# A graph layer on one core: the loop's buffers take fixed homes shared with the front, and the first one-hot matrices are built while the list goes through DRAM

## The chip, the cores and the metric

The kernel runs on one core of one Trainium2 chip. The metric is device time in microseconds of a whole execution. The engines are named as the profile names them: PE (matmuls; PEld loads their weights), DVE, ACT, POOL, and SP, which issues DMAs. A core has a PSUM memory of eight banks of 512 floats per partition, into which PE writes; DVE and ACT read it there. Everything else that the engines work on lies in SBUF.

## The reference

The layer takes 6250 nodes of 128 channels and 206,250 edges, sorted by their target node `dst`. It normalises the nodes, and for each node takes the largest message of its incoming edges:

```python
h = jnp.maximum(_layernorm(x, axis=-1), 0.0)
# for each edge (src, dst), with W = [W1 W2]:
feat = jnp.concatenate([h[dst], h[src] - h[dst]], axis=-1)
msg = feat @ W.T + b
out = jax.ops.segment_max(msg, dst, num_segments=6250)
x = x + jnp.where(jnp.isfinite(out), out, 0.0)
```

A message is a part that depends on `dst` alone plus a part `B[src]` that depends on `src` alone, so the kernel needs, for each node, the channelwise maximum of `B` over its neighbours.

## The kernel before

Nodes are numbered as `l * 50 + q`, with 125 values of `l` and `Q` = 50 of `q`. The lanes are the 128 partitions; a lane owns `LD` = 49 successive target nodes and looks at a window of `WIN` = 1792 edges. All order is written out by hand: the engines run their instructions in the order in which the code names them, and each engine waits, by semaphores, for the others where an instruction touches what another one wrote or read.

**The front** (lines 168 to 723) loads the windows, and does two things at once. It computes `B` (the small steps `turn`, `product` and `remainder` of `micro`, on PE and ACT, 75 in all for 25 pairs of `q`; `ln(n)` issues the next n of them), in two parts: `Bp` in SBUF, and `Bt` and `XA` in DRAM. And it marks the edges that a dense method cannot take: in the lag loop (lines 557 to 562) DVE compares the window with itself at 41 lags, and PE adds the results up in `dup`, four banks of PSUM (line 483); three result buffers `eq` take turns. `among[i]` lists what is issued after lag i. ACT takes the sign of `dup` (574), DVE scans it (585), and eleven passes (615 to 624) move the marked edges to the front of a list. `rest[i]` lists what is issued after pass i, among it `spread_a` and `spread_b` (where each lane's list goes), `turned` (PE transposes that make `TV`, `TD` and `TQ`) and `own_last`. The list is stored in DRAM as `LT` (666) and gathered back in two pieces (669, 670). What DVE does meanwhile is the product with `dup` of line 672, whose result becomes `TQ`, and tests whose results go to `badc`. Then `ridx` is made (696), and POOL begins to gather rows of `Bt` into `X`, a ring of `GB` = 12 groups.

**The way to the loop** (842 to 879). For each of 13 tiles of up to ten lanes there are two units (6 and 4 lanes). For a unit, `pieces` are six DVE comparisons and products that make one-hot matrices `OHQ` and `OHD` (755 to 762) from `TQ`, `TD` and `TV`; `mats` are 14 small PE matmuls for each two lanes, into `pv` (792). `square` (ACT, 801 to 804) makes `Vb` and `Vf` of `pv`. Before the loop stand the pieces and matmuls of units 0 and 1, `put_own(0)` (rows of `Bt`, turned by PE and copied to `acc` by ACT), `square(0)` and the pieces of unit 2.

**The loop** (937 to 974) has 325 pairs: 13 tiles of 490 columns (the last 392), with 25 pairs of `q` each. For a pair, `one_hots` makes two or three one-hot matrices: PE computes `z` (874), ACT makes `oh` of it (875). PE multiplies them with `Bp` into the pair's `ps`, two banks, with four or six matmuls (949), and DVE takes the maximum of `ps` and `acc2` into `acc2` (955). `ps` comes from a pool with two buffers (733). Beside this DVE runs the stream (159: a maximum over the gathered rows, 396 steps, a little over one in a pair), the pieces of later units, and PE the `pv` matmuls of later units, as `plan` says. The PSUM of the loop: three banks of `z`, four of `ps`, one of `pv`; that of the front: four of `dup`, two of `pt`, two of `pm`. Pools are opened for the front (170 to 172) and, after it, for the loop (732 to 734).

**The end** (983 to 996) turns `acc`, takes the maximum with the rows `R` gathered from the stream and stores the sum with x.

Of the kernel before, what the change touches and what calls it, by code (L numbers as in the profile page):

```python
# [12 lines left out]
I32 = mybir.dt.int32  # L13
# [42 lines left out]
def gnn_kernel(tc, x, src, dst, W, b, out):  # L56
# [35 lines left out]
    with ExitStack() as ctx:  # L92
# [14 lines left out]
        with ExitStack() as body:  # L107
# [30 lines left out]
            none = keep.tile([P, C], F32, name="none")  # L138

# [28 lines left out]
            with ExitStack() as pre:  # L168
                pool = pre.enter_context(tc.tile_pool(name="pre", bufs=1))
                ps_d = pre.enter_context(tc.tile_pool(name="ps_d", bufs=1, space=PSUM))  # L170
                ps_t = pre.enter_context(tc.tile_pool(name="ps_t", bufs=2, space=PSUM))
                ps_m = pre.enter_context(tc.tile_pool(name="ps_m", bufs=2, space=PSUM))
                dup = ps_d.tile([P, WIN], F32, name="dup")
# [47 lines left out]
                spare = acc[:1, 4 * GQ * C:]  # L221
# [8 lines left out]
                frow = spare[:, 256:256 + 2 * C].rearrange("o (r c) -> o r c", r=2)  # L230
# [7 lines left out]
                KA = pool.tile([P, 64 + WIN], I16, name="KA")  # L238
                KB = pool.tile([P, 64 + WIN], I16, name="KB")
                dlc_ = pool.tile([P, 64 + WIN + 2], BF16, name="dlc_")  # L240
# [40 lines left out]
                swin = pool.tile([P, WIN + 8], I32, name="swin")  # L281
                dwin = pool.tile([P, WIN], I32, name="dwin")
                big = pool.tile([P, WIN], F32, name="big")
# [33 lines left out]
                p = ps_m.tile([P, 512], F32, name="pm")  # L317
# [28 lines left out]
                kk = pool.tile([P, NS], F32, name="kk")  # L346
# [28 lines left out]
                def spread_begin():  # L375
                    p = ps_t.tile([P, 2 * P], F32, name="ptb", tag="pt")
                    T_.matmul(p[:1, :P], begin, ident, start=True, stop=True)
                    spread["p"] = p
# [14 lines left out]
                bs = spare[:, 512:512 + 3 * P - 1]  # L393
# [11 lines left out]
                def turn(k):  # L405
                    pt = ps_t.tile([P, 2, P], F32, name="pt")
# [8 lines left out]
                def product(k):  # L415
                    pm = steps[k]["pm"] = ps_m.tile([P, 2, 2 * C], F32, name="pm")
# [34 lines left out]
                vm = pool.tile([P, WIN], BF16, name="vm")  # L451
                q16 = pool.tile([P, WIN], BF16, name="q16")
                q2 = eq[2].bitcast(I16)
                gk = KB[:, 64:]
                d16 = pool.tile([P, WIN], I16, name="d16")
                s16 = pool.tile([P, WIN], I16, name="s16")
# [40 lines left out]
                own = pool.tile([P, WIN], BF16, name="own")  # L497
# [36 lines left out]

                among = {i: [] for i in range(SH + 1)}
                among[5] += [lambda: A_.copy(KB[:, 64:], KA[:, 63:63 + WIN])]
# [18 lines left out]
                for i in range(1, 35):  # L555
                    among[i].append(lambda: ln(1))
# [21 lines left out]
                less = junk[0]  # L578
                V.tensor_tensor(less[:, 1:], d16[:, 1:], d16[:, :WIN - 1], ALU.is_lt)
                V.memset(less[:, :1], 0.0)  # L580
                ln(6)
# [11 lines left out]
                def spread_a():  # L593
                    p = ps_m.tile([P, 512], F32, name="pm")
                    T_.matmul(p[:1, :P], nres, ident, start=True, stop=True)
                    V.tensor_scalar_add(rows[:, 0, :P], p[:1, :P], -float(GR))
                    V.memset(rows[:, 1], 0.0)
                    V.memset(rows[:, 4], 0.0)
                    V.tensor_tensor_scan(rows[:, 1, 2:], rows[:, 0, :P], rows[:, 4, :P], 0.0, op0=ALU.add, op1=ALU.max)
                    V.tensor_tensor(rows[:, 2, :P], lrow, rows[:, 1, 1:P + 1], ALU.subtract)  # L600
                    V.scalar_tensor_tensor(rows[:, 3, :P], lrow, float(GR - ST), rows[:, 1, :P], op0=ALU.add,
                                           op1=ALU.subtract)
                    V.tensor_scalar_max(rows[:, 3, :P], rows[:, 3, :P], 0.0)

                def spread_b():
                    p = ps_m.tile([P, 512], F32, name="pm")
                    for j, r in enumerate((2, 3, 1)):
                        o = 1 if r == 1 else 0
                        T_.matmul(p[:, j:j + 1], rows[:, r, o:o + P], ones[:1, :1], start=True, stop=True)
                    V.tensor_copy(cols_, p[:, :2])  # L610
                    V.tensor_copy(over_, p[:, 2:3])

                mask = big.bitcast(I32)

                def pass_(i):
                    s = 1 << i
                    parts = ((0, WIN - s),)
                    if s == 512:
                        parts = ((0, NS), (1024, min(1024 + NS, WIN - s)))
                    elif s == 1024:  # L620
                        parts = ((0, NS),)
                    for a, z in parts:
# [36 lines left out]
                for i in range(11):  # L659
                    pass_(i)  # L660
                    for f in rest[i]:
                        f()
# [409 lines left out]
```

## Time and profile before

| | us |
|---|---|
| median of three runs | 807.34 (806.42 to 807.71) |
| the profiled execution | 807.11 |
| its span (first to last instruction) | 805.2 |
| DVE: first lag's comparison | from 31.57 |
| ACT: first sign of `dup` | from 101.61 |
| SP: store of the list | from 147.78 |
| DVE: the gathered list is read | from 154.62 |
| PE: first `ps` matmul of the loop | from 174.45 |
| DVE: last step of the loop (965) | from 779.85 |
| mean granted clock of PE | 0.959 |

Times within the span count from its first instruction. The two us between span and execution lie around it. A row of the timeline gives start, length, engine, line, operation, output and input, and in brackets how long the engine had been idle before it and what ended that.

### The profile page before, as it was taken

How to read it: one execution, taken by the hardware profiler on the slowest of the kernel's cores; microseconds unless marked ns; L12 is line 12 of the kernel's file. 1: busy time of each engine (PE TensorE's matmuls, PEld its weight loads, DVE VectorE, ACT ScalarE, POOL GpSimd, SP SyncE). 2: the span in 40 equal slices, each digit the busy share in tenths (PEclk: the TensorE clock that was granted, in tenths of full speed). 3: DMA queues.
4: the chain of work that ended last, by engine and by line, in shares of the span. 5: the costliest groups of instructions: out<-in, count | busy, mean ns of one | idle time of the engine just before them, and what ended most of it. 6: DMA issues, size and time to landing. Idle time of an engine off the chain costs nothing.

```text
span 805.2 us, 12657 instructions
## 1 busy us (share of the span) xinstructions
PE 689.9 (86%) x3875; PEld 517.3 (64%) x3882; DVE 723.1 (90%) x1274; ACT 541.0 (67%) x1163; POOL 452.7 (56%) x489
## 2 busy tenths in 40 slices
PE   1697956579999898998989899998989999899992
PEld 0354534357677676776767677676767767677881
DVE  7999989869999888999999989999998999997976
ACT  4553467446899999567676767777776777777740
POOL 3000000377767377666667677777777777777270
PEclk9999999769999998999999999999999999999997
DMA  6420122323335833333333333433434343333385
GB/s 188 128 65 4 61 65 65 116 62 83 92 104 120 203 98 88 97 93 104 92 83 106 94 107 96 108 99 96 110 96 111 96 108 99 102 103 98 84 208 160
DMA packets 81692, 82.38 MB, mean 102 GB/s; under 512 B 11756, under 2 KB 69731, under 8 KB 81362
## 3 DMA queue, kind: packets, MB, share of 16 engines
q1 hardware_dynamic: 65741, 46.02, 20.2%
q0 software_dynamic: 15312, 34.57, 17.3%
q10 hardware_dynamic: 564, 0.92, 0.4%
q8 instruction: 32, 0.52, 0.3%
q14 instruction: 43, 0.35, 0.1%
HBM read 45.39 MB, written 39.19 MB: 105 GB/s over the span
## 4 chain that ended last, share of the span: by engine, by line
PE 56%; DVE 21%; ACT 13%; issue 6%; DMA 2%; POOL 0%; SPq 0%; DVEq 0%; ACTq 0%; POOLq 0%
PE ps L949 31%; PE z L874 14%; PE pv L792 7%; ACT oh L875 6%; DVE T L494 4%; DVE acc L955 3%; DVE dwin L624 2%; ACT Vb L802 1%; ACT dump L969 1%; ACT Vb L801 1%; DVE big L623 1%; DVE X L159 1%; ACT Vf L804 1%; DVE stats L294 1%; PE pm L420 1%
## 5 line engine op out<-in xcount | busy, mean ns | idle before, releaser
L86 POOL DMA_INDIRECT X<-Bt,ridx x396 | 393.9, 995 | 159.4 <-issue 44.8
L875 ACT ACTIVATE oh<-z 126x490 fp32r<-126x490 f32 (+1 forms) x754 | 381.1, 578 | 149.8 <-PE z L874 148.1
L949 PE MATMUL ps<-oh,Bp 126*128 126x490 f32 (+1 forms) x1508 | 445.1, 423 | 7.7 <-DVE acc L955 6.8
L955 DVE TENSOR_TENSOR acc<-acc,ps 128x980 f32<-128x980 f32 (+1 forms) x312 | 360.0, 1154 | 49.8 <-PE ps L949 45.0
L949 PEld LDWEIGHTS ps<-oh,Bp 126*128 126x128 f32 x1508 | 285.2, 192 | 107.9 <-DVE acc L955 36.4
L874 PE MATMUL z<-Vb,Sel 128*126 128x490 f16 (+1 forms) x650 | 195.8, 375 | 29.0 <-ACT oh L875 25.7
L159 DVE SCALAR_TENSOR_TENSOR X<-X,slim 128x128 f32<-128x128 f32 x395 | 136.2, 345 | 0.6
L874 PEld LDWEIGHTS <-Sel 128*126 128x126 f16 x754 | 100.6, 141 | 41.5 <-issue 6.6
L86 POOL DMA_INDIRECT swin<-LT,cols__955 x2 | 1.9, 956 | 135.6 <-DVE own_n L684 135.3
L792 PEld LDWEIGHTS <-OHQ 128*128 128x128 bf16 x910 | 62.4, 163 | 18.0 <-issue 17.2
L792 PE MATMUL pv<-OHD,OHQ 128*128 128x28 bf16 (+1 forms) x896 | 67.1, 228 | 4.6 <-DVE X L700 4.5
L86 POOL DMA_INDIRECT R<-M,last_e x49 | 47.5, 969 | 30.3 <-issue 20.5
L755 DVE TENSOR_TENSOR OHQ<-T,IQ 128x1092 bf16<-128x1092 bf16 (+5 forms) x104 | 61.6, 600 | 0.0
L483 PE MATMUL dup<-T,identb 128*128 128x512 bf16 (+1 forms) x159 | 39.4, 371 | 9.3 <-DVE T L494 8.7
L874 PE MATMUL z<-Vf,Sel 128*126 128x490 f16 (+1 forms) x104 | 38.9, 374 | 0.5 <-ACT Vf L804 0.5
L420 PE MATMUL pm<-wT,hT 128*125 128x256 f32 x100 | 30.0, 426 | 7.5 <-ACT hT L409 7.4
L969 ACT ACTIVATE dump<-lane_dl,nbias 128x472 bf16<-128x472 int32 x50 | 36.1, 721 | 0.0
L483 PEld LDWEIGHTS <-identb 128*128 128x128 bf16 x164 | 15.9, 101 | 25.4 <-issue 13.3
L420 PEld LDWEIGHTS pm<-wT,hT 128*125 128x125 f32 x100 | 19.7, 207 | 14.0 <-ACT hT L409 11.5
L403 ACT ACTIVATE hs<-X,nmr,rstd 125x128 f32<-125x128 f32 x50 | 22.1, 495 | 0.5 <-DVE nmr L306 0.5
L624 DVE COPY_PREDICATED dwin<-big,dwin 128x472 int32<-128x472 int32 (+10 forms) x12 | 21.8, 1813 | 0.4
L953 DVE TENSOR_TENSOR acc<-ps,acc 128x980 f32<-128x980 f32 (+1 forms) x13 | 15.1, 1163 | 7.7 <-PE ps L949 6.1
(266 smaller groups left out, 468.6 us busy)
## 6 DMA issues: line engine op xcount, KB each, us to landing
M<-X SPq DMA_DIRECT2D x198, 128.0 KB
X<-Bt,ridx POOLq DMA_INDIRECT x396
XA<-in_x POOLq DMA_DIRECT2D x1, 3125.0 KB
ownb<-Bt SPq DMA_DIRECT2D x12, 245.0 KB
X<-in_x SPq DMA_DIRECT2D x5, 560.0 KB
Bt<-acc SPq DMA_DIRECT2D x5, 560.0 KB
XA<-acc SPq DMA_DIRECT2D x5, 560.0 KB
out_x<-R SPq DMA_DIRECT2D x10, 224.0 KB
```

The lines of the kernel that those rows point to most:

```text
L86: G_.indirect_dma_start(out=o, out_offset=None, in_=table, in_offset=bass.IndirectOffsetOnAxis(ap=idx, axis=0))
L159: V.scalar_tensor_tensor(G[:, j], state["prev"], slim[:, k:k + 1], G[:, j], op0=ALU.min, op1=ALU.max)
L420: T_.matmul(pm[:L, j], hT[k % 2][:, j, :L], wT, start=False, stop=j == 1)
L483: T_.matmul(dup[:, c0:c1], w, e[:, c0:c1], start=first, stop=last)
L624: V.copy_predicated(pk[:, a:z], mask[:, a:z], pk[:, a + s:z + s])
L755: V.tensor_tensor(OHQ[:, :nl, a:z], over(TQ, z - a), iq, ALU.is_equal)
L792: T_.matmul(o, w, m, start=False, stop=True, skip_group_check=True)
L874: T_.matmul(z[:L + 1, :n], Sel[:, order[i // 2][j]], f[t % 2][:, :n], start=True, stop=True)
L875: A_.activation(oh[:, :n], z[:L + 1, :n], AF.Relu)
L949: T_.matmul(ps[:, j, :n], w, o[:, :n], start=m == 0, stop=m == len(todo) - 1)
L955: V.tensor_tensor(a, a, ps[:, :, :n], ALU.max)
L969: A_.activation(dump, lane_dl, AF.Sign, scale=2.0, bias=nbias[:, c:c + 1], accum_out=ends[:, c:c + 1])
```

## The change

The instructions are nearly the same ones (POOL has two memsets that DVE had); their places and order change.

- **Homes.** `psd`, one tile of four banks, holds `dup` in the front and, in the loop, the `ps` of a pair: the first two banks for even pairs, the last two for odd ones. Four tiles of one bank serve as `pt` and `pm` in the front, as `z` (three, in turn) and `pv` in the loop, and at the end. `HOT` holds `KA`, `KB`, `vm`, `q16`, `own` and `dlc` in the front and all one-hot matrices in the loop; `R` holds the window and the list in the front. The pools `ps_d`, `ps_t`, `ps_m`, `ps_z`, `ps_s`, `ps_v`, `hot`, `Rp` and `ps_f` go.
- **The lag loop** issues one small step after each lag from 1 to 40, and two after lags 12, 16, 20 and so on to 40 (before: one after lags 1 to 34). `rising` (lag 7; before it stood after the loop as `less`) and `near_ends` (lag 14; before it stood beside the list's gathers) come into it.
- **After it**, the product with `dup` stands ahead of the scan, and is made in place in `q16`. In the passes, `spread_a` stands ahead of the small steps, and all twelve `turned` are spread over the passes 0 to 5, `own_last` over 6 and 7.
- **While the list goes through DRAM**, DVE makes the pieces of units 0 and 1 and PE multiplies them; the tests that stood there come later. Only `square(0)` and the pieces of unit 2 stand before the loop.
- **In the loop**, `put_own(0)` and its load move in (pairs 8 and 20 for the first two tiles), so that the first pair's maximum is with a constant, and `acc` of the first tile comes in at the tile's end. Two groups of gathers, not one, are issued in each of the first pairs.

```diff
+            psd = psb.tile([P, 4, 512], F32, name="psd")
+            banks = [psb.tile([P, 512], F32, name=f"bank{i}") for i in range(4)]
...
+            OHQs = [hot_piece(m, SQ) for m in (UL, TL - UL)]
...
+            vm, q16, own = (HOT[:, 2 * KW + i * WIN:2 * KW + i * WIN + WIN] for i in range(3))
...
+            swin = R2[:, :WIN + 8].bitcast(I32)
...
-                dup = ps_d.tile([P, WIN], F32, name="dup")
+                dup = psd.rearrange("p a b -> p (a b)")[:, :WIN]
...
+                def rising():
+                    flush(0)
+                    e = eq[used["n"] % 3]
+                    used["n"] += 1
+                    V.tensor_tensor(e[:, 1:], d16[:, 1:], d16[:, :WIN - 1], ALU.is_lt)
+                    V.memset(e[:, :1], 0.0)
+                    A_.activation(e, e, AF.Copy, accum_out=badc[:, 0:1])
...
+                among[7] += [rising]
+                among[14] += [near_ends]
...
-                for i in range(1, 35):
-                    among[i].append(lambda: ln(1))
+                for i in range(1, SH):
+                    among[i].append(lambda i=i: ln(2 if i > 8 and i % 4 == 0 else 1))
...
-                less = junk[0]
-                V.tensor_tensor(less[:, 1:], d16[:, 1:], d16[:, :WIN - 1], ALU.is_lt)
-                V.memset(less[:, :1], 0.0)
-                ln(6)
+                V.scalar_tensor_tensor(q16, dup, float(SG), q16, op0=ALU.mult, op1=ALU.add)
+                ln(2)
...
+                rest[0].append(spread_a)
+                rest[2].append(spread_b)
+                for i in range(8):
+                    rest[i].append(lambda i=i: ln(4 if i < 7 else len(micro)))
+                for h in range(4):
+                    for i, (t, to) in enumerate(((q16, TQ), (vm, TV), (dlc, TD))):
+                        rest[(3 * h + i) // 2].append(lambda h=h, t=t, to=to: turned(t, to, h))
+                    rest[6 + h // 2].append(lambda h=h: own_last(h))
...
                 S_.dma_start(LT.rearrange("(p s) o -> p (s o)", p=P), pk[:, :ST])
+                for o in OHQs:
+                    G_.memset(o[:, :, Q:], 0.0)
...
                 gather(first, LT[:, :], cols_[:, 1:2])
...
+                for u_ in (0, 1):
+                    for f in pieces(u_):
+                        f()
+                    mats(u_, 0, UL)
...
-                    ps = ps_s.tile([P, 2, 512], F32, name="ps")
+                    ps = psd[:, k % 2 * 2:k % 2 * 2 + 2]
...
-                    if i == 0:
+                    if k == 0:
+                        V.tensor_scalar_max(a, ps[:, :, :n], -FMAX)
+                    elif i == 0:
```

How the built programs stand at three places. The first is PE in the loop, in the first tile: `ps_` with a number is one buffer of the pool, `z_` and `bank` the PSUM of `z`; an instruction's waits are the engines' semaphore counts in brackets. Before:

```order
L949 MATMUL ps_1916<-oh_1873,Bp_76 128x490 [waits DVE_49]
L949 MATMUL ps_1916<-oh_1873,Bp_76 128x490
L949 MATMUL ps_1916<-oh_1877,Bp_76 128x490 [waits Activation_49]
...
L874 MATMUL z_1929<-Vb0_84,Sel_77 126x490 [waits Activation_49]
...
L949 MATMUL ps_1937<-oh_1909,Bp_76 128x490 [waits DVE_49]
```

And after:

```order
L959 MATMUL psd_110<-oh_1750,Bp_76 128x490 [waits DVE_49]
L959 MATMUL psd_110<-oh_1750,Bp_76 128x490
L959 MATMUL psd_110<-oh_1753,Bp_76 128x490 x2
...
L884 MATMUL bank2_113<-Vb0_84,Sel_77 126x490 [waits Activation_49]
...
L959 MATMUL psd_110<-oh_1764,Bp_76 128x490 [waits DVE_49]
```

Two successive pairs write `ps_1916` and `ps_1937` before, and `psd_110` both times after (its two halves). The first matmul of a pair waits for a count of DVE in both.

The second place is DVE between the lag loop and the scan (`T3` holds the signs). Before:

```order
L502 TENSOR_TENSOR T3_83<-dlc__181 128x1792 [waits DVE_49,PE_49]
L260 TENSOR_TENSOR Sel_77<-wmask_152,wrow_151 128x2520
L569 MEMSET swin_217 128x1
L570 MEMSET pos_h_904 128x1
L579 TENSOR_TENSOR KA_179<-d16_338 128x1791 [waits DVE_49]
L585 SCALAR_TENSOR_TENSOR swin_217<-T3_83,ones_93 128x896 [waits Activation_49]
```

And after:

```order
L520 TENSOR_TENSOR T3_83<-HOT_106 128x1792 [waits DVE_49,PE_49]
L288 TENSOR_TENSOR Sel_77<-wmask_152,wrow_151 128x2520
L605 MEMSET R_105 128x1
L606 MEMSET pos_h_938 128x1
L614 SCALAR_TENSOR_TENSOR HOT_106<-psd_110,HOT_106 128x1792 [waits PE_49,Activation_49]
L619 SCALAR_TENSOR_TENSOR R_105<-T3_83,ones_93 128x896 [waits DVE_49]
```

The comparison `less` (579) has left this place, and the product with `dup` (614) has come in ahead of the scan (585, now 619), with a wait for ACT of its own.

The third place is DVE after the list's store (`lane_dl` reads the list; `badc` holds the tests; the copy under a mask reads the gathered list). Before:

```order
L676 TENSOR_SCALAR lane_dl_91<-dwin_218 128x472
L678 TENSOR_SCALAR swin_217<-kk_303,over__101 128x136
L680 TENSOR_SCALAR badc_92<-nres_952 128x1
...
L691 TENSOR_TENSOR badc_92<-badc_92,body_m_309 128x1
...
L695 COPY_PREDICATED swin_217<-swin_217 128x136
```

And after:

```order
L759 TENSOR_SCALAR lane_dl_91<-R_105 128x472
L761 TENSOR_SCALAR R_105<-R_105,over__101 128x136
L643 TENSOR_TENSOR HOT_106<-T3_83,IQ_80 128x6x182 x2
...
L647 TENSOR_TENSOR HOT_106<-T3_83,IW_81 128x1176
...
L650 TENSOR_TENSOR HOT_106<-HOT_106,T3_83 128x784
L767 COPY_PREDICATED R_105<-R_105 128x136
```

The pieces of two units (643 to 650) stand where the tests stood, ahead of the copy.

More of the change, by code (lines that the diff above doesn't have):

```diff
@@ L605, in spread_b @@
[L605 to L622, printed above, removed]
-                        V.tensor_scalar(mask[:, a:z], pk[:, a + s:z + s], 2 << i, None, op0=ALU.bitwise_and)
-                        V.copy_predicated(pk[:, a:z], mask[:, a:z], pk[:, a + s:z + s])
@@ new lines, in turned @@
+                def turned(s, t, h):
+                    h0, h1 = h * 32, h * 32 + 32
+                    pt = bank("t")[:, :32 * NBLK].rearrange("p (a b) -> p a b", b=NBLK)
+                    for j in range(NBLK):
+                        T_.matmul(pt[:, :, j], s[:, j * P:(j + 1) * P], identb[:, h0:h1], start=True, stop=True)
+                    A_.copy(t[:, h0:h1], pt)
+                own_n = pool.tile([P, 4], F32, name="own_n")
+                obias = pool.tile([P, 1], F32, name="obias")
@@ L815, in put_own @@
                     c0 = tiles[t][0] * LD
[L816 removed]
+                    z = bank("z")
                     for k in range(cols[t] // 98):
```

303 lines of the change are left out of this document (146 added, 157 removed).

## The prediction

> **What bounds the kernel now.** I read the page first, then busy time by stage, then the order of time at the three places that the change touches. The page's chain that ended last, by line, and the groups of instructions that matter (count; busy us, mean ns of one; idle us before them and who ended it):
>
> ```profile
> PE ps L949 31%; PE z L874 14%; PE pv L792 7%; ACT oh L875 6%; DVE T L494 4%; DVE acc L955 3%; DVE dwin L624 2%; ACT Vb L802 1%; ACT dump L969 1%; ACT Vb L801 1%; DVE big L623 1%; DVE X L159 1%; ACT Vf L804 1%; DVE stats L294 1%; PE pm L420 1%
> L949 PE MATMUL ps<-oh,Bp 126*128 126x490 f32 (+1 forms) x1508 | 445.1, 423 | 7.7 <-DVE acc L955 6.8
> L955 DVE TENSOR_TENSOR acc<-acc,ps 128x980 f32<-128x980 f32 (+1 forms) x312 | 360.0, 1154 | 49.8 <-PE ps L949 45.0
> L159 DVE SCALAR_TENSOR_TENSOR X<-X,slim 128x128 f32<-128x128 f32 x395 | 136.2, 345 | 0.6
> L755 DVE TENSOR_TENSOR OHQ<-T,IQ 128x1092 bf16<-128x1092 bf16 (+5 forms) x104 | 61.6, 600 | 0.0
> ```
>
> PE's `ps` matmuls hold the largest share of the chain, and they waited 6.8 us for DVE in the whole program: the two engines work side by side. By stage (length; busy us of PE, PEld, DVE, ACT, POOL; granted clock; DMA):
>
> ```profile
> 72.00:98.80 26.80, 26.48 (x126) 15.00 (x127) 26.26 (x55) 12.79 (x37) 0.00 (x0) 0.96 0.15 48
> 101.60:109.00 7.40, 3.38 (x8) 1.96 (x8) 7.09 (x6) 5.44 (x13) 0.00 (x0) 0.77 0.04 3
> 122.00:143.00 21.00, 14.47 (x124) 10.29 (x126) 20.62 (x15) 14.78 (x45) 0.00 (x0) 1.00 0.19 62
> 169.00:175.00 6.00, 3.03 (x9) 1.58 (x8) 1.61 (x4) 5.41 (x11) 4.69 (x5) 0.50 0.31 87
> 174.40:779.90 605.50, 570.15 (x3172) 441.68 (x3170) 550.77 (x899) 451.35 (x936) 423.63 (x429) 0.98 0.40 105
> ```
>
> The loop (174.40 to 779.90) has PE 94% and DVE 91% busy, 1.86 us for each of its 325 pairs. That both can be so full in one stretch is owed to the two `ps` buffers, seen in order of time (start, length, engine, in brackets the idle time and its releaser):
>
> ```profile
> 182.44 1.67 PE L949 MATMUL ps<-oh,Bp 126*128 126x490 f32 x6
> 184.15 1.18 DVE L955 TENSOR_TENSOR acc<-acc,ps 128x980 f32<-128x980 f32 x1 [0.57 <-PE ps L949]
> ...
> 196.16 1.17 DVE L955 TENSOR_TENSOR acc<-acc,ps 128x980 f32<-128x980 f32 x1
> ...
> 197.38 1.15 PE L949 MATMUL ps<-oh,Bp 126*128 126x490 f32 x4 [0.33 <-DVE acc L955]
> 197.51 1.17 DVE L955 TENSOR_TENSOR acc<-acc,ps 128x980 f32<-128x980 f32 x1
> ...
> 198.73 1.60 PE L949 MATMUL ps<-oh,Bp 126*128 126x490 f32 x6
> ```
>
> The matmuls of 197.38 were released by the maximum that ran from 196.16, two pairs back, and ran beside the next maximum (197.51), which reads the other buffer.
>
> **The change, part by part. 1: `ps` becomes half of one tile.** `ps_s` with two buffers goes; a pair now takes one half of `psd`. The halves still alternate, but the program guards `psd` as one: counted through the built program, the DVE count for which a pair's first `ps` matmul waits is reached by the maximum of the pair before, in 323 of 325 pairs; before the change it was the maximum two pairs back, in 322. So 197.38 would have waited for the end of 197.51. PE may run `z` and `pv` beside a maximum, but no `ps` any more, and a pair becomes a closed round: matmuls, handover, maximum, handover.
>
> Its length follows from the rows above. Four matmuls take 1.15 when they start after a wait, six take 1.60; the maximum takes 1.17. The handover to DVE is 184.15 less the end of the matmuls (182.44 + 1.67), 0.04; that to PE is 197.38 less the end of the maximum (196.16 + 1.17), 0.05. Sums: 2.41 and 2.86. Of a tile's 25 pairs, 8 have three one-hots and six matmuls (4 + 4 of the 50 values of `q` are in `twos`), 17 have four. Twelve tiles: 12 × (17 × 2.41 + 8 × 2.86) = 766.2. The last tile has 392 columns:
>
> ```profile
> 771.62 1.37 PE L949 MATMUL ps<-oh,Bp 126*128 126x392 f32 x6
> 771.62 0.97 DVE L955 TENSOR_TENSOR acc<-acc,ps 128x784 f32<-128x784 f32 x1 [0.21 <-PE ps L949]
> ...
> 773.02 1.02 PE L949 MATMUL ps<-oh,Bp 126*128 126x392 f32 x4
> ```
>
> 17 × (1.02 + 0.97 + 0.09) + 8 × (1.37 + 0.97 + 0.09) = 54.8. Loop: 821.0 in place of 605.5, **+215.5**. DVE's other work (136.2 + 61.6 us of lines 159 and 755, 0.61 per pair) lies beside the 1.15 to 1.60 of matmuls; only where two steps of the stream and a piece meet (2 × 0.345 + 0.60 = 1.29) does it stick out. If that happened in every pair it would cost 325 × 0.14 = 46. PE's `z` and `pv` lie beside the maximum. If the wait for the tile took half of the handovers away, it would be 325 × 0.045 = 15 less. I take the sum itself.
>
> The Trainium skill, "PSUM — Partial Sum Buffer", section "PSUM bank collisions raise a hardware error", asks for a guard by bank, not by address; the rows at 197.38 and 197.51 agree that two engines may work in different banks at once. By that rule a guard as wide as four banks is not needed, and a chip bound by banks alone would run the loop in the old 605.5; but the wait stands in the program, so that this is only a rival.
>
> **2: the list starts later.** Rows of the lag loop, of its end, and of what the list waits for:
>
> ```profile
> 84.78 0.92 PE L483 MATMUL dup<-T,identb 128*128 128x512 bf16 x4
> ...
> 87.10 0.38 ACT L425 COPY acc<-pm 125x256 f32<-125x256 f32 x1
> ...
> 88.74 0.92 PE L483 MATMUL dup<-T,identb 128*128 128x512 bf16 x4
> ...
> 92.70 6.06 PE L483 MATMUL dup<-T,identb 128*128 128x512 bf16 x28
> ...
> 98.84 0.92 PE L483 MATMUL dup<-T,two_i 128*128 128x512 bf16 x4
> ...
> 101.41 1.09 DVE L579 TENSOR_TENSOR KA<-d 128x1791 bf16<-128x1791 int16 x1
> ...
> 101.61 1.91 ACT L574 ACTIVATE T<-dup,pos_h 128x896 bf16<-128x896 f32 x2 [8.28 <-DVE pos_h L570]
> ...
> 102.65 2.02 DVE L585 TENSOR_TENSOR_SCAN swin<-T,ones 128x896 int32<-128x896 bf16 x1
> ...
> 115.27 0.28 DVE L596 TENSOR_SCALAR rows<-pm 1x128 f32<-1x128 f32 x1 [2.69 <-PE pm L595]
> ...
> 147.67 2.02 DVE L672 SCALAR_TENSOR_TENSOR s<-dup,q 128x1792 bf16<-128x1792 f32 x1
> ...
> 149.61 0.40 DVE L676 TENSOR_SCALAR lane_dl<-dwin 128x472 int32<-128x472 int32 x1
> ...
> 150.75 0.20 DVE L687 TENSOR_TENSOR fl<-dlc__181,IW 128x14 f32<-128x14 bf16 x1
> ...
> 151.56 0.16 DVE L691 TENSOR_TENSOR badc<-badc,body_m 128x1 f32<-128x1 f32 x1
> ```
>
> - `rising` and `near_ends` come into the lag loop, where DVE is full: 1.09 (row 101.41) and five tiny tests, 0.97 from 150.75 to 151.72, that stood beside the list's trip: +2.0.
> - The loop gets 48 small steps of the product for 34. Twelve of the new ones fall behind its 20th lag, where PE is full (26.48 of 26.80). Three lags and one product (three small steps) take 88.74 − 84.78 = 3.96; seven lags alone 6.06. So a product costs 3.96 − 3 × 0.87 = 1.36, and twelve steps 5.4. Two steps back to back also show PE's wait for ACT; its two copies (0.38 each, row 87.10) cannot cost more than 0.76 for each of four products, +3.0. I take 6.5. What hid PE's end before goes first: it was done at 99.76 (98.84 + 0.92), ACT began at 101.61: −1.8.
> - The `q16` product with `dup` (2.02, row 147.67) stood beside the list's trip and now stands before the scan; it also waits for both signs that ACT takes of `dup`. Scan after the first sign's start: 102.65 − 101.61 = 1.04 before, 1.91 + 2.02 + 0.04 now: +2.9.
> - `spread_a` now stands ahead of the small steps, so the 2.69 for L595 goes, all but some 0.2: −2.5.
>
> Sum: the list's store some **7 us later** (4 to 10).
>
> **3: the way from the list to the loop is shorter.**
>
> ```profile
> 147.78 0.35 SPq L666 DMA_DIRECT2D LT<-dwin  x1
> ...
> 154.62 0.32 DVE L695 COPY_PREDICATED swin<-swin 128x136 int32<-128x136 int32 x1 [2.27 <-DMA swin<-LT,cols__955]
> ...
> 159.76 2.49 DVE L755 TENSOR_TENSOR OHQ<-T,IQ 128x1092 bf16<-128x1092 bf16 x4
> ...
> 163.71 0.53 DVE L755 TENSOR_TENSOR OHQ<-T,IQ 128x728 bf16<-128x728 bf16 x1
> ...
> 166.60 2.55 DVE L755 TENSOR_TENSOR OHQ<-T,IQ 128x1092 bf16<-128x1092 bf16 x4
> 166.67 1.76 PEld L792 LDWEIGHTS <-OHQ 128*128 128x128 bf16 x27 [0.15 <-issue]
> ...
> 169.94 0.47 ACT L801 ACTIVATE Vb<-pv,shift_u 50x245 f16<-50x245 f32 x1
> ...
> 174.45 2.18 PE L949 MATMUL ps<-oh,Bp 126*128 126x490 f32 x4
> ```
>
> From store to first `ps` it is 26.7 now (174.45 − 147.78). After: 0.7 for `lane_dl` (0.40) and `moved` (a third as long, less than that), 6.9 for the pieces of two units (159.76 to 166.60), some 1.9 for the last 28 `pv` matmuls (27 of their loads take 1.76 from 166.67), and 4.5 from the first shift to the first `ps` (169.94 to 174.45): 14.0, **−12.7**. The list itself needs 6.84 (154.62 − 147.78), so the pieces cover it, by 0.8. POOL's two new memsets stand before the list's gathers; they need `own_last`, which now ends inside the passes, so the store's trip covers them (uncovered, an estimate of 1 us each by the nearest row of that width, the maximum's 1.17). Moved into the loop, the two copies into `acc` of the first tile are covered by PE's new waits; its one maximum more costs at most another 1.17, half as wide as it is. Front in all: 7 − 12.7 = **−5.7**, say −5 (−9 to −2).
>
> **The rivals.** *The guard lets go by bank after all*, as the skill's rule would have it: then only the front is left, 807.1 − 5 = **802**, faster. Against it stands the count in the program. Chance 0.05, of which 0.01 for a front that gains nothing that can be told.
>
> *PE's clock falls.* It idles in every round. At 0.50 (169.00:175.00) four matmuls took 2.18; six would be 3.03 by the same ratio. Rounds of 3.44 and 4.29 make the twelve tiles 1113 and the last some 80: about **1390**. Against it: in 122.00:143.00, with PE busy 69% in short pieces, the clock was 1.00; in a round of 2.55 PE still works some 1.9. The Trainium skill, "TensorE: Matmul & The Clock Gate", section "A second HAM failure mode: psum-queue depth-cycling", tells of a clock that swings when PE idles between groups as it goes through banks. By it the time would lie between 1018 and 1390. The row 101.60:109.00 (46% busy, 0.77) shows that it can. Chance 0.05.
>
> *DVE's other work does not fit beside the matmuls.* If half of the 0.61 per pair stuck out, 325 × 0.3 = 99 more, **1117**. Against it: it needs 0.61 and finds 1.24 or 1.69. Chance 0.05.
>
> *The gather stream sets the pace* is no rival: POOL is 70% busy in the loop, and the stream, tied to pairs, slows with them.
>
> **How the numbers follow.** The profiled execution took 807.11, its span 805.2; the median is 807.34, the same to 0.03%. 807.1 + 215.5 − 5 = 1018. The range goes down by the handovers (15), the front (4) and 2% of 821 (16), since the rounds' lengths come from single rows, to 985 in round numbers, and up by the front (4), the 2% and half of the 46 to 1060; the forecast (0.85) nearly always lies in it, the rivals do not. A difference of 0.2% can be told from none: faster 0.04 and within 0.2% 0.01 (the first rival), slower 0.95.
>
> **What would show it.** Right: in the loop DVE's maximum waits for PE in every pair and the first `ps` matmul for the maximum just before it, never beside it; rounds of 2.4 and 2.9; PE and DVE busy near 70%; the loop some 820 long; clock near 1; first `ps` at 166 to 173. Wrong: `ps` matmuls that start while a maximum runs, or a clock of 0.8 or less in the loop, or rounds over 2.7 with DVE full.

## The result, and the profile after

The change makes the kernel slower: 1038.08 us in the median (1037.55 to 1039.28) against 807.53, a ratio of 1.2863 with an interval of 1.2838 to 1.2888. The profiled execution took 1039.28, its span is 1037.3. The kernel before, executed 28 times beside the later runs on two chips, took 806 to 811 us in 13 of them and 813 to 821 in 15, these at a lower mean clock (0.930 to 0.943 for 0.951 to 0.959), so that a ratio within some 1% of 1 has to be read with the rows. Of the 232.1 by which the span grew, the loop holds 230.9, the front 0.9 and the end 0.2:

| start, us | before | after |
|---|---|---|
| ACT: first sign of `dup` | 101.61 | 109.45 |
| DVE: first scan | 102.65 | 113.33 |
| SP: store of the list | 147.78 | 159.80 |
| PE: first `ps` matmul | 174.45 | 175.39 |
| DVE: last step of the loop | 779.85 | 1011.72 |
| loop, from one to the other | 605.4 | 836.3 |

In the new page line 959 is the `ps` matmul, 967 the maximum, 884 `z`; `psd` is the tile whose halves are `ps`. The chain that ended last, by line, and two groups:

```profile
PE psd L959 37%; DVE acc L967 25%; PE bank L680 5%; PE bank L884 3%; DVE T L513 2%; PE psd L502 2%; DVE R L713 1%; DVE acc L965 1%; PE bank L443 1%; DVE HOT L643 1%; DVE X L193 1%; DVE R L1007 1%; DVE R L712 1%; DVE stats L319 1%; DMA X<-Bt,ridx 1%
L959 PE MATMUL psd<-oh,Bp 126*128 126x490 f32 (+1 forms) x1508 | 421.6, 407 | 198.0 <-DVE acc L967 184.5
L967 DVE TENSOR_TENSOR acc<-acc,psd 128x980 f32<-128x980 f32 (+1 forms) x312 | 361.5, 1159 | 263.1 <-PE psd L959 261.2
```

The maximum, 3% of the chain before, is now 25% of it, in turn with the matmuls. PE waited 6.8 us for it before and 184.5 now, DVE 45.0 for PE before and 261.2 now. The same work takes as long as it did (407 and 1159 ns for one); it no longer lies side by side. By stage:

```profile
72.00:98.80 26.80, 24.79 (x117) 14.66 (x117) 22.94 (x53) 16.08 (x48) 0.00 (x0) 0.94 0.22 68
101.60:109.00 7.40, 6.66 (x34) 3.89 (x33) 5.99 (x6) 4.51 (x14) 0.00 (x0) 1.00 0.01 3
122.00:143.00 21.00, 18.52 (x122) 13.54 (x122) 17.33 (x20) 11.26 (x31) 0.00 (x0) 0.53 0.19 61
175.40:1012.00 836.60, 634.91 (x3175) 417.76 (x3175) 568.28 (x909) 457.52 (x936) 428.12 (x443) 0.99 0.30 78
```

In the loop (the last row) PE is busy 76% (94 before) and DVE 68% (91 before), at a clock of 0.99. The third row is one to keep: the clock was 0.53 in the passes, 1.00 before. The loop in order of time, matmuls and maxima alone:

```profile
315.09 1.15 PE L959 MATMUL psd<-oh,Bp 126*128 126x490 f32 x4 [0.65 <-DVE acc L967]
316.28 1.18 DVE L967 TENSOR_TENSOR acc<-acc,psd 128x980 f32<-128x980 f32 x1 [0.98 <-PE psd L959]
...
317.51 1.60 PE L959 MATMUL psd<-oh,Bp 126*128 126x490 f32 x6 [0.85 <-DVE acc L967]
...
319.15 1.18 DVE L967 TENSOR_TENSOR acc<-acc,psd 128x980 f32<-128x980 f32 x1 [0.72 <-PE psd L959]
...
320.38 1.15 PE L959 MATMUL psd<-oh,Bp 126*128 126x490 f32 x4
```

The matmuls of 317.51 begin 0.05 after the end of the maximum of 316.28, which is the one just before; that maximum began 0.04 after the end of its own matmuls. Rounds of 2.42 and 2.87 follow, and no `ps` matmul runs beside a maximum.

### The profile page after: what moved, and what is told of

It reads as the page before. It is cut to its first block, busy times and chain, and to the rows that moved or that the text cites. A ratio compares the mean times of both kernels' runs of the same rounds, so it can differ in the third digit from the quotient of the medians.

```text
span 1037.3 us, 12652 instructions
## 1 busy us (share of the span) xinstructions
PE 760.6 (73%) x3882; PEld 496.7 (48%) x3882; DVE 738.6 (71%) x1273; ACT 548.0 (53%) x1163; POOL 444.7 (43%) x491
## 3 DMA queue, kind: packets, MB, share of 16 engines
q1 hardware_dynamic: 65741, 46.02, 15.6%
## 4 chain that ended last, share of the span: by engine, by line
PE 49%; DVE 40%; issue 6%; DMA 3%; ACT 1%; POOL 0%; SPq 0%; DVEq 0%; POOLq 0%; ACTq 0%
PE psd L959 37%; DVE acc L967 25%; PE bank L680 5%; PE bank L884 3%; DVE T L513 2%; PE psd L502 2%; DVE R L713 1%; DVE acc L965 1%; PE bank L443 1%; DVE HOT L643 1%; DVE X L193 1%; DVE R L1007 1%; DVE R L712 1%; DVE stats L319 1%; DMA X<-Bt,ridx 1%
## 5 line engine op out<-in xcount | busy, mean ns | idle before, releaser
L885 ACT ACTIVATE oh<-bank 126x490 fp32r<-126x490 f32 (+1 forms) x754 | 384.5, 574 | 359.8 <-PE bank L884 358.9
L959 PE MATMUL psd<-oh,Bp 126*128 126x490 f32 (+1 forms) x1508 | 421.6, 407 | 198.0 <-DVE acc L967 184.5
L967 DVE TENSOR_TENSOR acc<-acc,psd 128x980 f32<-128x980 f32 (+1 forms) x312 | 361.5, 1159 | 263.1 <-PE psd L959 261.2
L959 PEld LDWEIGHTS psd<-oh,Bp 126*128 126x128 f32 x1508 | 261.2, 190 | 364.4 <-DVE acc L967 314.3
L884 PE MATMUL bank<-Vb,Sel 128*126 128x490 f16 (+1 forms) x650 | 191.4, 373 | 3.2 <-ACT oh L885 3.1
L680 PEld LDWEIGHTS <-HOT 128*128 128x128 bf16 x910 | 62.5, 162 | 21.7 <-issue 21.0
L680 PE MATMUL bank<-HOT 128*128 128x28 bf16 (+2 forms) x910 | 67.3, 228 | 7.6 <-DVE HOT L650 7.5
L643 DVE TENSOR_TENSOR HOT<-T,IQ 128x1092 bf16<-128x1092 bf16 (+5 forms) x104 | 61.8, 601 | 0.0
L513 DVE TENSOR_TENSOR T<-HOT 128x1792 bf16<-128x1792 int16 x41 | 43.3, 1078 | 5.6 <-PE psd L502 5.5
L502 PE MATMUL psd<-T,identb 128*128 128x512 bf16 (+1 forms) x164 | 39.6, 369 | 6.0 <-DVE T L513 5.9
```

The source lines that it names most:

```text
L502: T_.matmul(dup[:, c0:c1], w, e[:, c0:c1], start=first, stop=last)
L513: V.tensor_tensor(e, KA[:, 64:], i1, ALU.is_equal)
L643: V.tensor_tensor(OHQ[:, :nl, a:z], over(TQ, z - a), iq, ALU.is_equal)
L680: T_.matmul(o, w, m, start=False, stop=True, skip_group_check=True)
L884: T_.matmul(z[:L + 1, :n], Sel[:, order[i // 2][j]], f[t % 2][:, :n], start=True, stop=True)
L885: A_.activation(oh[:, :n], z[:L + 1, :n], AF.Relu)
```

## The experiments

On the chip of the first four runs the kernel before took 991 us in the median. The traces of these four runs show engines standing still, for up to 12.6 us at a time, without a cause in the program; the kernel before was only timed there. Of these four only rows are used which such a standstill does not touch, and two kernels were run again elsewhere.

**Two homes.** The theory is the guard: `psd` is one tile, so the program holds a pair's matmuls back until the maximum of the pair before has read the other half. The edit gives `ps` two buffers again; the tile `psd` is closed after the front.

```diff
-            psd = psb.tile([P, 4, 512], F32, name="psd")
+            psdx = ExitStack()
+            psd = psdx.enter_context(tc.tile_pool(name="psdp", bufs=1, space=PSUM)).tile([P, 4, 512], F32, name="psd")
...
+                psdx.close()
+                ps_s = mid.enter_context(tc.tile_pool(name="ps_s", bufs=2, space=PSUM))
...
-                    ps = psd[:, k % 2 * 2:k % 2 * 2 + 2]
+                    ps = ps_s.tile([P, 2, 512], F32, name="ps")
```

> The changed kernel, but ps again comes from a pool of its own with two buffers; all else of the change stays. Theory A (the one guard over psd makes a pair a closed round, and nothing else in the change costs much): the front of the changed kernel (first ps matmul at 175.4), the loop of the kernel before (605.5) and its end (25.4) give a span of 806.3, a time of 808, range 802 to 814; the first ps matmul of a pair waits for the maximum two pairs back, PE is again over 90% busy in the loop. Theory B (something else that the change puts into the loop, or the clock of TensorE, makes the rounds long): the time stays above 950.

Measured 984.94, against 991.28 of the kernel before beside it. The waits of that run (us in total, times, longest) show the standstills, put down to "issue" and "remote", to no instruction of this core:

```profile
PEld L888 <- issue: 102.4, 76, 8.7
ACT oh L889 <- remote: 100.1, 17, 10.8
```

By its number it would have spoken for theory B; beside a kernel before that is as slow it tells nothing. Again:

> two_homes once more, since on the chip of the first four runs the kernel before took 991 in place of 807, its engines standing for 3 to 9 us at a time without a releaser in the program. Theory A (the one guard over psd is what the change costs): first ps matmul at 175 to 176, a loop of 605 to 610, time 806 to 812. Theory B (something else of the change makes the loop long): above 950 on a chip where the kernel before takes 807.

808.18, the kernel before 815.29 beside it: 0.9925 (0.9882 to 0.9968). The loop in order of time (these rows are of the fastest of its twelve executions, 801.58):

```profile
171.61 1.97 PE L963 MATMUL ps<-oh,Bp 126*128 126x490 f32 x4
...
194.16 1.16 DVE L971 TENSOR_TENSOR acc<-acc,ps 128x980 f32<-128x980 f32 x1
...
195.37 1.17 PE L963 MATMUL ps<-oh,Bp 126*128 126x490 f32 x4 [0.31 <-DVE acc L971]
195.51 1.16 DVE L971 TENSOR_TENSOR acc<-acc,ps 128x980 f32<-128x980 f32 x1
...
774.45 0.57 DVE L984 TENSOR_TENSOR acc<-acc 128x392 f32<-128x392 f32 x1
```

The matmuls of 195.37 run beside the maximum of 195.51 and were released by that of 194.16, two pairs back. From the first `ps` matmul the loop is 602.8 long, 605.4 before, with PE busy 94% of it. The first `ps` matmul and the loop both came earlier than theory A gave, the time inside its range. Theory A holds: the one line on `ps` carries all of the loss. Whether the rest of the change gains is not shown by these times: the ratio is 0.75% below 1, and the kernel before took anything from 807.42 to 819.50 beside it.

**One home.** The kernel before with that line alone, and the tile that it needs:

```diff
-                ps_s = mid.enter_context(tc.tile_pool(name="ps_s", bufs=2, space=PSUM))
+                ps_s = mid.enter_context(tc.tile_pool(name="ps_s", bufs=1, space=PSUM))
+                psd = ps_s.tile([P, 4, 512], F32, name="psd")
...
-                    ps = ps_s.tile([P, 2, 512], F32, name="ps")
+                    ps = psd[:, k % 2 * 2:k % 2 * 2 + 2]
```

> The kernel before, with one edit: ps is a half of one tile of four banks, by turns, in place of two buffers of a pool; nothing else of the change. Theory A: the loop takes the 836.9 of the changed kernel in place of 605.5, with the front of the kernel before (first ps matmul at 174.5): 807 + 231 = 1038, range 1028 to 1046; rounds of 2.42 and 2.87. Theory B (the shared guard alone does not do it): 807, or a part of the 231.

On the first chip 1092.51. Its rounds were those of the changed kernel nevertheless:

```profile
207.97 1.18 DVE L956 TENSOR_TENSOR acc<-acc,psd 128x980 f32<-128x980 f32 x1 [0.99 <-PE psd L950]
...
210.40 1.18 DVE L956 TENSOR_TENSOR acc<-acc,psd 128x980 f32<-128x980 f32 x1 [0.99 <-PE psd L950]
...
213.27 1.18 DVE L956 TENSOR_TENSOR acc<-acc,psd 128x980 f32<-128x980 f32 x1 [0.28 <-PE psd L950]
```

2.43 and 2.87 from one maximum to the next. Elsewhere:

> one_home once more, for the same reason. Theory A: rounds of 2.42 and 2.87 with few that are longer, a loop of 833 to 840, time 1035 to 1044. Theory B: 807, or a part of the way.

1043.89, ratio 1.2823 (1.2702 to 1.2943), inside what theory A gave. The loop's ends:

```profile
184.41 2.18 PE L950 MATMUL psd<-oh,Bp 126*128 126x490 f32 x4
...
1019.52 0.57 DVE L966 TENSOR_TENSOR acc<-acc 128x392 f32<-128x392 f32 x1
```

835.1, within 1.2 of the changed kernel's loop. One tile in place of two is enough to make it. The first `ps` matmul, though, came 10 us later than in the kernel before, in the same order of instructions; to that below.

**Four matmuls in each pair.** If a pair is a closed round, taking two matmuls out of the rounds with six must shorten exactly these. This kernel leaves the third one-hot's product out of the sum:

```diff
-                        todo = [(Bp[:, e, q], o) for o, q in oh[j] for e in range(2)]
+                        todo = [(Bp[:, e, q], o) for o, q in oh[j][:1] for e in range(2)]
```

> The changed kernel with four ps matmuls in every pair: in the 104 pairs with three one-hots the third one's two matmuls are left out of the sum, its z and oh are still made. Theory A (closed rounds): 96 rounds of 2.87 become 2.42 and the last tile's 8 of 2.40 become 2.05: 96 x 0.45 + 8 x 0.35 = 46 less, time 992, range 988 to 997. Rival F (ACT's one-hots or the gather stream hold the longer rounds open anyway): less than half of that, above 1015.

997.86, 0.9 above the range that theory A gave and far below rival F's 1015; the loop, from 174.63, ended with the row

```profile
970.04 0.57 DVE L980 TENSOR_TENSOR acc<-acc 128x392 f32<-128x392 f32 x1
```

and is 795.4 long, 40.9 less. That is 89% of the 46. Of the 5.1 that are missing, 4.0 are rounds that ran over their size (the usual length of their kind) by more than 0.1: 29 rounds, by 15.6 in all, against 24 rounds and 11.6 in the changed kernel. The model holds, rival F falls.

**Six small steps before the scan.** In the front PE stood behind the matmul of `spread_a`, and DVE later waited for `spread_b`. On top of two_homes:

```diff
-                ln(2)
+                ln(6)
                 for a in (0, HW):
```

> two_homes, and six small steps of the product instead of two between the signs and the scan. Theory C (in the changed kernel PE stands behind the matmul of spread_a from 112.8 to 119.8, the granted clock falls to 0.50 until 141, and the slow PE makes DVE wait 3.3 for spread_b): four more steps of 1.1 fill that gap, the clock stays above 0.9 from 120 to 140, the wait of 3.3 goes, and the list's store and the first ps matmul come 3 to 4 us earlier than in two_homes; time 3 to 4 us below it. Theory D (DVE waits for spread_b because 56 matmuls of the turned tables now stand ahead of it in PE's queue, whatever the clock): the wait keeps 1.5 us or more, and the gain is at most 2.

987.55 on the first chip. PE's wait and DVE's:

```profile
121.05 0.59 PE L686 MATMUL bank<-ident,nres 128*1 128x128 f32 x2 [2.66 <-DVE obias L737]
...
135.19 0.16 DVE L701 CAST cols__987<-bank 128x2 int32<-128x2 f32 x1 [2.36 <-PE bank L700]
```

PE's wait went from 7.04 to 2.66, yet the clock still was 0.50 from 120 to 130, and 2.36 of 3.3 stayed; the list's store came 1.1 earlier than in two_homes on the same chip (159.01 against 160.08). Theory C fails as it was put, D gets its numbers right. But two_homes_2 had this:

```profile
119.63 0.58 PE L686 MATMUL bank<-ident,nres 128*1 128x128 f32 x2 [7.04 <-DVE obias L737]
...
120.00:124.00 4.00, 3.58 (x10) 2.15 (x8) 3.90 (x7) 1.75 (x6) 0.00 (x0) 0.54 0.00 0
124.00:128.00 4.00, 2.75 (x36) 2.08 (x36) 3.90 (x6) 3.24 (x9) 0.00 (x0) 1.00 0.64 197
...
131.83 0.16 DVE L701 CAST cols__967<-bank 128x2 int32<-128x2 f32 x1 [0.46 <-PE bank L700]
```

The same queue and the same standstill of 7.04, but the clock back at 124, and the wait is 0.46. Four traces have this front: with the clock back at 124, 130, 141 and 141 us (two_homes_2, four_each, the changed kernel, two_homes) the wait is 0.46, 1.36, 3.29 and 3.26. So the matmuls ahead of `spread_b` make it late as long as the clock is low, against theory D's "whatever the clock", and when the clock comes back does not follow from the length of the standstill, which was 7.04 in all four.

**The lag loop's small steps as before.** On top of steps_early, one step after each of the lags 1 to 34:

```diff
-                for i in range(1, SH):
-                    among[i].append(lambda i=i: ln(2 if i > 8 and i % 4 == 0 else 1))
+                for i in range(1, 35):
+                    among[i].append(lambda: ln(1))
```

> steps_early, and the lag loop again gives out one small step at each of the lags 1 to 34 (34 steps, where the change has 48); the passes take the other 14. Theory C': in the changed kernel DVE waits 5.5 us for PE among the lags, against 0.5 before; these 5 us go, the fourteen steps fit into the passes beside DVE, and the store and the first ps matmul come 4 to 6 us earlier than in steps_early: 7 to 10 us earlier than in two_homes, time 798 to 801 if that is at 808. Rival E: the passes then hold more of PE's work than DVE's 37 us cover, and what is saved among the lags is waited for there: within 1.5 us of steps_early.

983.07 on the first chip. In this kernel the low parts of the last two values of `q` come out other than in the change: two sums of `own_last`, in the same two banks by turns, now stand on PE (155.4 to 157.2) between the last `product` and its `remainder` (158.02). The instructions are the same. The last comparison of the lag loop began 5.3 earlier than in steps_early (100.61 against 105.95), without a wait for PE ahead of it. The list was ready 6.1 earlier (152.92 against 158.99), but its store was not:

```profile
158.83 0.75 SPq L463 DMA_DIRECT2D XA<-acc  x2
159.67 1.05 SPq L754 DMA_DIRECT2D LT<-R  x1
...
160.37 2.55 DVE L645 TENSOR_TENSOR HOT<-T,IQ 128x1092 bf16<-128x1092 bf16 x4 [6.81 <-ACT HOT L735]
```

The store stood on SP behind the last group's `XA`, which waited for the last small step. And DVE, ahead of the pieces (645), waited 6.81 for ACT's last sign of `own_last` (735), which stands behind the small steps too. Theory C' holds for the lags and not for what follows. Rival E gets its number right, the first `ps` matmul 1.2 later than in steps_early; what was saved is waited for just behind the passes, by DVE and on SP.

**A front put in another order.** Two_homes with one small step at each lag, six before the scan, and:

```diff
-                V.scalar_tensor_tensor(q16, dup, float(SG), q16, op0=ALU.mult, op1=ALU.add)
...
+                V.scalar_tensor_tensor(q16, dup, float(SG), q16, op0=ALU.mult, op1=ALU.add)
                 V.tensor_tensor(pk, pk, u[:, :WIN], ALU.bitwise_or)
...
-                rest[2].append(spread_b)
+                rest[1].append(spread_b)
...
                 oh = one_hots(*pairs[0])
+                z = bank("z")
+                T_.matmul(z[:P - 1, :1], ident[:, 1:], heads[:, 1:], start=True, stop=True)
+                V.tensor_copy(mend_i[:P - 1], z[:P - 1, :1])
```

> two_homes with the front's queues put in another order: one small step of the product at each lag (40, not 48) and six before the scan (not two); the product q16 with dup behind the second scan, so that the first scan waits for one sign alone; spread_b ahead of the other work of its pass; the matmul of heads behind the first z. By the trace of the changed kernel: of the 5.5 us that DVE waits for PE among the lags 4 go, 0.9 before the scan, 3 of the 3.3 at spread_b, 1 of PE's 2.5 at heads. Theory: the list's store at 151 to 153, the first ps matmul at 165 to 168, time 8 to 10 us below two_homes, and below the kernel before by over 1%. Rival: the small steps moved out of the lags are waited for in the passes, the store comes 4 us earlier at most, and the time is within 0.5% of the kernel before.

802.01, 0.9859 (0.9797 to 0.9921): 6.2 below two_homes_2 where 8 to 10 were expected, and all six executions below the fastest of the kernel before (807.42). The list's store came at 149.73, 6.5 earlier than in two_homes_2 and earlier than expected, the first `ps` matmul only at 168.96, 2.6 earlier and later than expected. A new wait had come:

```profile
168.22 0.15 DVE L893 CAST mend_i<-bank 127x1 int32<-127x1 f32 x1
168.43 0.57 PE L885 MATMUL bank<-Vb,Sel 128*126 128x490 f16 x1 [2.45 <-DVE mend_i L893]
```

The bank of `heads` was the next `z`'s, and the copy that frees it stands behind DVE's pieces. So the next kernel moves it, and gives `ps` two tiles with fixed homes:

```diff
-                z = bank("z")
+                z = banks[3]
...
+                ps_ = [ps_s.tile([P, 2, 512], F32, name=f"ps{i}") for i in range(2)]
...
-                    ps = ps_s.tile([P, 2, 512], F32, name="ps")
+                    ps = ps_[k % 2]
```

> fit with two edits. The matmul of heads goes to the bank of pv and no longer takes a z buffer: in fit the next z waited 2.45 us for DVE's copy mend_i, which stands behind 3.9 us of pieces; that wait goes, and the first ps matmul comes 2 to 2.5 us earlier (166.5). And ps takes two tiles of two banks each by turns, each with a fixed home, in place of a pool that hands out two buffers. Theory G (what counts is that two pairs' tiles are guarded apart, not that a pool rotates them): the loop stays at 603 to 608, time 2 us below fit. Rival H (fixed homes wait longer than rotated ones): a loop of over 640.

800.40, 0.9869 (0.9807 to 0.9930), 1.6 below fit. PE no longer waits for `mend_i`:

```profile
167.84 1.97 PE L964 MATMUL ps<-oh,Bp 126*128 126x490 f32 x4
...
770.11 0.57 DVE L985 TENSOR_TENSOR acc<-acc 128x392 f32<-128x392 f32 x1
```

The loop is 602.3 with fixed homes: theory G holds, rival H falls. What counts is two tiles, not a pool that rotates them. The first `ps` matmul came 1.1 earlier than in fit, not 2 to 2.5, but the list's store was 2.3 later (152.02).

The last kernel issues the last group's store to `XA` behind the list's:

```diff
-                        for to, j in ((Bt_l, g), (XA_l, 2 + g)):
+                        for to, j in ((Bt_l, g), (XA_l, 2 + g))[:1 if q0 + GQ == Q else 2]:
...
                 S_.dma_start(LT.rearrange("(p s) o -> p (s o)", p=P), pk[:, :ST])
+                for p0, p1 in PARTS:
+                    S_.dma_start(XA_l[p0:p1, Q - GQ:], stage[p0:p1, 2 + (Q // GQ - 1) % 2])
```

> fit_heads, and the last group's store to XA (two DMAs, 1.5 us of SP's queue) is issued behind the list's store, not 2 us ahead of it. In fit the gathered list was there 10.0 us after its store was issued, 8.5 in the changed kernel, where that group's store had gone out 9 us earlier. Theory: DVE's wait of 1.2 for the list goes and the first ps matmul comes up to 1 us earlier than in fit_heads. Rival: the path to the first ps matmul goes over PE's pv matmuls and ACT's shifts, not over the list: within 0.3 us of fit_heads.

797.01, 0.9839 (0.9784 to 0.9894), the fastest kernel of the study. But the rows are against its theory: from the list's store (151.38) to the first `ps` matmul it took 15.84, in fit_heads 15.82, and in neither did DVE wait for the list (in fit it had, 1.18). The first `ps` matmul came 0.6 earlier than in fit_heads, as the store itself did.

```profile
151.38 0.35 SPq L755 DMA_DIRECT2D LT<-R  x1
...
160.01 0.32 DVE L772 COPY_PREDICATED R<-R 128x136 int32<-128x136 int32 x1
...
167.22 1.97 PE L966 MATMUL ps<-oh,Bp 126*128 126x490 f32 x4
```

The 3.4 between the two medians has no cause that was shown, and the two intervals overlap.

## Why the prediction was right, and what it missed

It said 1018 (985 to 1060) by a closed round behind one guard. The direction, the mechanism and its place were right; the time was 20 too low. Of the span's 21.6, 15.3 is the loop's (836.3 for 821.0) and 5.9 the front's: +0.9 in place of −5, outside its own range of −9 to −2, with the first `ps` matmul at 175.39 and not at 166 to 173.

**The guard and the round: right.** Handovers of 0.04 and 0.05, rounds of 2.42 and 2.87 for 2.41 and 2.86. With these sizes, and 54.0 for the last tile's 25 rounds, the forecast's own sum is 12 × (17 × 2.42 + 8 × 2.87) + 54.0 = 823.2, where it said 821.0.

**DVE's other work taken as hidden: mis-sized.** The sum took 0 of a bound of 46. It also counted that work short: line 755 is not all of the pieces, lines 759 and 762 add 29.7 us in the loop before. Of the 324 rounds, 24 are longer than their size by more than 0.1, 11.6 in all. In 15 of these, 6.2 of it, DVE came late to the maximum, as here with a piece (650) between two steps of the stream (193):

```profile
301.95 1.16 PE L959 MATMUL psd<-oh,Bp 126*128 126x490 f32 x4
...
302.49 0.35 DVE L193 SCALAR_TENSOR_TENSOR X<-X,slim 128x128 f32<-128x128 f32 x1
...
302.75 0.76 DVE L650 TENSOR_TENSOR HOT<-HOT,T 128x1176 bf16<-128x1176 bf16 x1
...
303.44 0.34 DVE L193 SCALAR_TENSOR_TENSOR X<-X,slim 128x128 f32<-128x128 f32 x1
...
303.70 1.17 DVE L967 TENSOR_TENSOR acc<-acc,psd 128x980 f32<-128x980 f32 x1
```

The matmuls ended at 303.11, the maximum began at 303.70. Ten of the 15 are such a meeting of the stream and the pieces, as the prediction named it; four stand at a tile's last steps; the largest, 1.3, is a row of small tests (lines 924 to 938) that stand in the loop. The rival in which half of this work sticks out falls: it would have cost 99. In a closed round each such delay lengthens the loop, since no second buffer takes it up.

**The clock: right as a whole, wrong in places.** It was 0.99 in the loop. But four rounds had matmuls of 2.0 in place of 1.15, or 2.7 to 2.8 in place of 1.60, 4.0 in all:

```profile
592.29 2.69 PE L959 MATMUL psd<-oh,Bp 126*128 126x490 f32 x6 [0.85 <-DVE acc L967]
```

From 591 to 596 the clock was 0.66. One of the four is the second pair's, at the loop's start (clock 0.51 from 175 to 183). The Trainium skill, "TensorE: Matmul & The Clock Gate", section "A second HAM failure mode: psum-queue depth-cycling", has the clock swing where PE idles between groups and goes through banks. The trace bears that out in three rounds of 324 and not as a state of the loop, though PE idled 24% of it. Three rounds in which the matmuls began late and two just behind slow ones make the other 1.4 of the 11.6. Of the 1.5 of the loop that is left, 1.0 is the first pair, whose matmuls took 1.97 at the low clock and whose maximum came 0.25 after them; the rest is not accounted for.

**The guard by bank, a rival: not what the program does.** The Trainium skill, "PSUM — Partial Sum Buffer", section "PSUM bank collisions raise a hardware error", asks for a guard by bank. In two_homes_2 PE wrote two banks while DVE read two others, as its rows show: the trace agrees. The changed kernel waited since its program guards by tile: one_home has the wait, and fit_heads, with two tiles in fixed homes, has not.

**The list's store: 12.0 later, said 7 (4 to 10).** These are rows of the changed kernel:

```profile
109.45 1.91 ACT L610 ACTIVATE T<-psd,pos_h 128x896 bf16<-128x896 f32 x2 [0.89 <-PE psd L502]
...
111.38 2.02 DVE L614 SCALAR_TENSOR_TENSOR HOT<-psd,HOT 128x1792 bf16<-128x1792 f32 x1 [2.85 <-ACT T L610]
...
113.33 2.02 DVE L619 TENSOR_TENSOR_SCAN R<-T,ones 128x896 int32<-128x896 bf16 x1
...
119.83 0.58 PE L684 MATMUL bank<-ident,nres 128*1 128x128 f32 x2 [7.04 <-DVE obias L735]
...
134.86 0.16 DVE L699 CAST cols__964<-bank 128x2 int32<-128x2 f32 x1 [3.29 <-PE bank L698]
```

The first sign came 7.8 later; 2.0 + 6.5 − 1.8 = 6.7 were forecast. From it to the scan it took 3.88 in place of 1.04, +2.8, forecast 2.9. Up to here the steps hold. From scan to store the sum has −2.5, "`spread_a` now stands ahead of the small steps, so the 2.69 for L595 goes". The 2.69 went, but the stretch came out +1.3 (46.47 for 45.13). PE, which had small steps to do, stood 7.04 behind that matmul; its clock was 0.50 from 116 to 141, and its late work ahead of `spread_b` made DVE wait 3.29. **What failed is a term that the sum put at nothing: PE's clock in the passes, taken as before, and with it the wait at `spread_b`.** In two_homes_2, where PE stood 7.04 as well but the clock was back at 124, the stretch took 43.12, which is −2.0, near the forecast's −2.5:

```profile
156.25 0.35 SPq L754 DMA_DIRECT2D LT<-R  x1
```

That store is 8.5 later than in the kernel before, inside 4 to 10. So the 12.0 is an execution in which the clock came back late, and no run here shows what decides that.

**From the store to the first `ps`: 15.6, said 14.0.** The forecast's way to the first shift holds:

```profile
169.22 0.47 ACT L818 ACTIVATE Vb<-bank,shift_u 50x245 f16<-50x245 f32 x1 [12.75 <-PE bank L680]
...
171.65 0.59 PE L790 MATMUL bank<-heads,ident 128*127 128x1 f32 x2 [2.53 <-DVE heads L788]
172.10 1.06 PE L884 MATMUL bank<-Vb,Sel 128*126 128x490 f16 x2
```

159.80 + 0.7 + 6.9 + 1.9 = 169.3. Behind it the matmul of `heads` stands ahead of `z` in PE's queue and waits for DVE; the prediction did not count that queue. From the first shift to the first `z` it is 2.88, 1.97 in the kernel before. In fit_heads, where `heads` stands behind the first `z`, it is 1.96, and first shift to first `ps` is 5.1 (162.73 to 167.84) in place of 6.2; 4.5 were forecast. Two_homes_2 had the first `ps` matmul 2.8 earlier than the kernel before: of the −5 (−9 to −2) that was forecast for the front somewhat over half is there, in the fastest of its executions.

## What to carry to other kernels

Two halves of one tile are two buffers in memory and one in the guard: count, in the built program, which instruction a wait is reached by, and if it is the one just before, price the pair as a closed round of matmuls, handover, reader and handover. Give each buffer a tile of its own; fixed homes cost nothing then. And when an instruction that waits is moved ahead of ready work in an in-order queue, look at what stands behind it: here `heads` on PE cost 0.9 us, a store to `XA` on SP held back a list that was ready for 6.7 us (steps_back), and `spread_a` on PE made DVE wait up to 3.3 later on, where the clock stayed low.

## What was not expected of the hardware

A low clock of PE goes with some 7 us of the front, in one and the same order of instructions. One_home_2 has the front of the kernel before, whose store came at 147.78 with the clock at 0.95 to 1.00 from 108 to 148. Its own rows:

```profile
116.00:120.00 4.00, 3.67 (x10) 2.16 (x10) 1.20 (x6) 1.94 (x7) 0.00 (x0) 0.50 0.00 0
...
118.73 0.28 DVE L596 TENSOR_SCALAR rows<-pm 1x128 f32<-1x128 f32 x1 [5.25 <-PE pm L595]
...
130.10 0.16 DVE L610 CAST cols__955<-pm 128x2 int32<-128x2 f32 x1 [2.82 <-PE pm L609]
...
155.54 1.19 SPq L666 DMA_DIRECT2D LT<-dwin  x1
```

The clock was 0.50 from 104 to 141 although PE was busy 92% in the window shown, and the store came 7.8 later. Of this 0.9 was there at the first sign; DVE's waits for PE are 8.07 where the kernel before has 2.69, 5.4 more; and the store stood 1.5 on SP behind the last group's `XA`, which PE's late work had delayed. The other traced execution of this kernel, one_home, has the same low clock to 140 and waits of 5.09 and 2.82. When the clock returns (124, 130 and 141 in one order of instructions) is left open: no run here separates its cause. A difference of a few us in such a front is therefore read from the rows and their clock, not from one execution's time.
